# A later place in the planned order for two of GpSimd's products in a fused attention and state-space kernel

## The chip, the core and the metric

The kernel runs on one core of a Trainium2 chip. The metric is the device time of one execution in microseconds (us), the median of three runs. The core's engines are called by the profile's names: PE is TensorE (matmuls and transposes; PEld its weight loads), DVE is VectorE, ACT is ScalarE, POOL is GpSimd, SP is SyncE, which here issues the DMAs. Each engine works through its own instructions strictly in the order in which they were written; an instruction whose inputs are not there holds up all that stand behind it on its engine.

## The reference

The input is a batch of 8 images of 56 x 56 points with 192 channels. Two residual layers follow each other. The first is an attention layer over the points, with depthwise convolutions in front. The second, in which nearly all the time goes, is a selective state-space layer:

```
x = x + L0_conv(_gn(x))                       # group norm, convolutions, 3-head attention
x = x + L1_conv(_gn(x))                       # group norm, then for each image:
  xz = in_proj(x); xa, z = split(xz)          # 384 channels each
  xc = silu(conv3x3(xa))
  4 directions over the 3136 points (rows, columns, and both backwards), per direction:
    dts, Bs, Cs = split(x_proj(u))            # 12 + 16 + 16 rows
    delta = softplus(dt_proj(dts) + bias)
    for every point l, every channel, every one of 16 states n:
      h = exp(delta * A[n]) * h + delta * u * B[n, l]
      y = sum over n of h[n] * C[n, l]
  y = layernorm(sum of 4 directions) * silu(z); out_proj(y)
```

## The kernel before, in words

**The tiles.** An image is cut into 7 chunks of 448 points (T = 448), the 384 channels into 3 blocks of 128 (NJ = 3). With 8 images and 4 directions there are 8 x 4 x 7 = 224 chunk steps, and with 16 states each 3584 pairs (i, n) of a chunk step i and a state n. All of it is float32.

**What happens to one pair (i, n).** POOL multiplies `du`, the product of delta and u for the chunk, by a row of B that a DMA has spread over the partitions: this makes the input tile `h` of 128 x 1344 (`inputs_made`, L1127). ACT makes the three decays `da` (`decays`, L1141). DVE runs three scans along the points, in place in `h` (`scans`, L1158), and a small reduction copies the last column into `newc`, the carry for the next chunk (`carries`, L1180). Then `h` has to be multiplied by a row of C and added up over the states, and this is done in one of two ways:

- For 11 of the 16 states (13 in the last image) PE turns `h` (`turned`, L1204), ACT scales it by columns of C while it leaves PSUM (`scaled`, L1220), and PE turns it back and adds it up in the PSUM tile `y` (`back`, L1238).
- For the others POOL does it (`by_pool`): three products of `h` with the row of C, `cb`, one per channel block (L1257). `BY_POOL` puts the states in groups: (2, 5), (8, 10), (13) in the first seven images and (2, 7), (12) in the last. The first of a group writes its product into the tile `yp`; the next multiplies in place and POOL adds it to `yp` (L1261). PE then adds `yp` to `y` (`summed`, L1276). There is one `yp`.

At the end of a chunk step DVE adds `y` into `yacc` (`evicted`, L1293). There are seven buffers for `h` (`HBUFS = 7`), two for `du`, for delta and for `cb`, five for the rows of B, two for `da`.

**delta and u.** `prepared` makes delta for the next chunk step with PE, ACT and DVE (L1067 to L1086, the last one L1086, three times). Then POOL multiplies it into `du` (L1090), once per chunk step, and the chunk step is entered in `chunks`, on which the generators of the row loads, of the decays and of the inputs wait.

**Beside the scans** run the front of the next image (attention, projections, convolutions: `front`, `x_proj`) and the end of the last one (`finish`, with one POOL product at L988 per chunk). The front of the first image runs alone, before the first scan.

**What sets the order.** A list scheduler (`Sched`) plays the program in a model while the instructions are written. Every activity is a generator that asks for (engine, cost, cells read, cells written). The model knows when each cell was written, and with `LATE` how long after an instruction's end it can be used. Among all that could go next it takes the one with the smallest start less rank (`run`), and writes the instruction. The start is the latest of the stage's own start, its inputs and what is still read of its outputs, plus `HOP` = 0.04, and of the time at which the engine is free. The ranks are 0.39 for `by_pool`, 0.3 for `prepared`, 0.0 for `inputs_made`. The model's times steer only the order: on the chip each instruction waits for semaphores, and nothing else.

Where PE would be idle in the model for more than 0.45 us while `y` is being added up, the scheduler writes filler matmuls by `zeros` into an unused part of `y` (`keep_busy`, L1372), which keep PE's clock up; each counts 0.225 us in the model and each is an instruction that the chip carries out.

Of the kernel before, what the change touches and what calls it, by code (L numbers as in the profile page):

```python
# [10 lines left out]
ALU = mybir.AluOpType  # L11
# [10 lines left out]
T = 448  # L22
# [12 lines left out]
NJ = DIN // 128  # L35
# [18 lines left out]
PE, ACT, DVE, POOL, SP = range(5)  # L54
LATE = (0.17, 0.08, 0.09, 0.06, 0.0)
HOP = 0.04
MARGIN = 3.0
URGENT = 0.9


# [4 lines left out]
def t_mm(n):  # L65
    return n * 0.00171
# [6 lines left out]
def t_act(n):  # L73
    return 0.17 + n * 0.00085


def t_dve(n):
    return 0.07 + n * 0.00105


def t_pool(n):
    return 0.13 + n * 0.00214
# [82 lines left out]
class Sched:  # L165
# [17 lines left out]
    def resume(self, s, value=None):  # L183
        was, self.now = self.now, s
        try:
            s.req = s.gen.send(value)
        except StopIteration:
            s.done, s.req = True, None
        self.now = was

    def join(self, stages):

        me = self.now
        yield lambda: all(s.done for s in stages)
        me.start = max([me.start] + [s.end for s in stages])
# [7 lines left out]
    def give(self, s, t):  # L203
# [5 lines left out]
        if s.group is not None and e == PE:  # L209
            self.spent[s.group] = self.spent.get(s.group, 0.0) + cost  # L210
        end = t + s.req[4] + MARGIN if len(s.req) > 4 else end + LATE[e]
        for c in reads:
# [6 lines left out]
    def run(self, until=None):  # L219
        while True:  # L220
# [20 lines left out]
            for s in self.stages:  # L241
# [3 lines left out]
                if s.group in self.limit:  # L245
# [4 lines left out]
                    if spent < must:  # L250
                        rank = URGENT
                e, _, reads, writes = s.req[:4]
# [21 lines left out]
def kernel(  # L274
# [24 lines left out]
    nc = tc.nc  # L299
# [108 lines left out]
    sc = Sched()  # L408
# [57 lines left out]
    def dma(reads, writes, late, dst, src, after=()):  # L466
        yield SP, 0.07, reads, writes, late
        nc.sync.dma_start(dst, src)
        for t in after:
            t.free()  # L470
# [569 lines left out]
    chunks, brow, crow, das, states, news, ys = {}, {}, {}, {}, {}, {}, {}  # L1040
# [4 lines left out]
    def prepared():  # L1045

        for i, (b, k, c, _) in enumerate(steps):
            yield lambda: b in made and (k, c) in made[b]["k_ct"] and (k, c) in made[b]["k_rows"]
            m = made[b]
            cols = slice(c * T, (c + 1) * T)  # L1050
            dts = yield rdts[k // 2]
            yield from dma([m["k_rows"][k, c]], dts.c, 2.9, dts.ap[k // 2 * 64 + 1:k // 2 * 64 + 1 + R, :],
                           m["rows"][k][0:R, cols])
            ct = yield s2("ct_s", [TP, SUB, NST])
            yield from dma([m["k_ct"][k, c]], ct.c, 1.8, ct.ap, m["ct"][k][:, c * SUB:(c + 1) * SUB])
            dl = yield s2("dl_s", [128, NJ, T], parts=NJ)
            du = yield s2("du_s", [128, NJ, T], parts=2)
            yield from dma(m["k_xcs"][k % 2][c], du.c[:1], 5.5, du.ap, m["xcs"][k % 2][:, :, cols])


            for j in range(NJ):
                e = yield s2("e", [128, T])
                pdt = yield rprep
                k1, free = [Cell() for _ in range(3)], Cell()
                free.w = e.c[0].r
                yield PE, t_mm(T), dts.c, pdt.c
                nc.tensor.matmul(pdt.ap[:, :T], dtw[:, k % 2, j * 128:(j + 1) * 128], dts.ap,  # L1067
                                 start=True, stop=True)
                yield ACT, t_act(T), pdt.c + [free], [k1[0]]
                nc.scalar.activation(e.ap, pdt.ap[:, :T], AF.Abs)  # L1070
                yield ACT, t_act(T), [k1[0]], [k1[1]]
                nc.scalar.activation(e.ap, e.ap, AF.Exp, scale=-1.0)
                yield DVE, t_dve(T), pdt.c + [k1[1]], [k1[2]]
                nc.vector.scalar_tensor_tensor(dl.ap[:, j], pdt.ap[:, :T], 0.0, e.ap, ALU.max, ALU.add)  # L1074
                pdt.free()
                u = yield rprep
                k2 = [Cell() for _ in range(2)]
                yield ACT, t_act(T), [k1[1]], u.c + e.c
                nc.scalar.activation(u.ap[:, :T], e.ap, AF.Identity, bias=one)
                e.free()  # L1080
                yield DVE, t_dve(T), u.c + [k1[2]], [k2[0]]
                nc.vector.scalar_tensor_tensor(dl.ap[:, j], u.ap[:, :T], -1.0, dl.ap[:, j], ALU.add, ALU.subtract)  # L1082
                yield ACT, t_act(T), [k2[0]], [k2[1]]
                nc.scalar.activation(u.ap[:, :T], u.ap[:, :T], AF.Ln)
                yield DVE, t_dve(T), [k2[1], k2[0]], [dl.c[j]]
                nc.vector.tensor_tensor(dl.ap[:, j], u.ap[:, :T], dl.ap[:, j], ALU.subtract)  # L1086
                u.free()
            dts.free()
            yield POOL, t_pool(NJ * T), dl.c + du.c[:1], du.c[1:]
            nc.gpsimd.tensor_tensor(du.ap, dl.ap, du.ap, ALU.mult)  # L1090
            chunks[i] = (dl, du, ct)

    def skips():
# [72 lines left out]
    def over(i, n):  # L1166
        s = states[i, n]
        s[1] -= 1
        if s[1] == 0:
            states.pop((i, n))[0].free()  # L1170
# [73 lines left out]
    def by_pool():  # L1244

        for i, n in todo:
            if n not in by[i]:
                continue
            yield lambda: (i, n) in states and (i, n) in crow and i in news
            h, cbr = states[i, n][0], crow.pop((i, n))  # L1250
            first, last = by[i][n]
            if first:
                yp = yield s1("yp", [128, NJ, T], parts=NJ)
            to = yp if first else h
            for j in range(NJ):
                yield POOL, t_pool(T), [h.c[1 + j], news[i].c[n]] + cbr.c, [to.c[j]] if to is yp else [h.c[1 + NJ + j]]
                nc.gpsimd.tensor_tensor(to.ap[:, j], h.ap[:, j], cbr.ap, ALU.mult)  # L1257
            cbr.free()
            if to is h:
                yield POOL, t_pool(NJ * T), h.c[1 + NJ:] + yp.c, yp.c  # L1260
                nc.gpsimd.tensor_tensor(yp.ap, yp.ap, h.ap, ALU.add)  # L1261
            over(i, n)
            if last:
                yps.append((i, yp))
# [33 lines left out]
    with tc.manual_schedule():  # L1298
# [11 lines left out]
        with ExitStack() as es:  # L1310
# [15 lines left out]
            for g, rank in ((prepared, 0.3), (skips, 0.0), (row_loads, 0.25), (inputs_made, 0.0), (decays, 0.37),  # L1326
                            (scans, 0.16), (carries, 0.36), (turned, 0.37), (scaled, 0.38), (by_pool, 0.39),
                            (back, 0.4), (summed, 0.0), (evicted, 0.71)):
                sc.spawn(g(), rank, "scan")
# [114 lines left out]
```

## Time and profile before

| | us |
|---|---|
| median of three runs (18645.85 to 18656.8) | 18655.95 |
| span of the profiled execution, first to last instruction | 18641.6 |
| POOL busy | 16430.8 |
| PE busy (fillers of L1372: 1708.4 of it) | 16947.4 |
| DVE busy | 14715.5 |
| ACT busy | 14638.2 |
| mean granted PE clock, share of full | 0.978 |

The profile is of one execution. Its span is 14.4 us under the median of the runs, which also hold what lies around the instructions. Busy times are per engine and overlap; PE's are drawn out by the modelled ends of its matmuls. In a group of instructions the last column is the idle time of the engine just before them and what ended most of it. "A <- B" in a list of waits says that engine line A sat idle until B released it; "issue" as the releaser means that the profile shows nothing that it waited for.

### The profile page before, as it was taken

The page shows a single profiled execution, that of the slowest core. Times are in us where ns is not written, and L with a number is a line of the kernel's source. Part 1 is how long each engine was busy: PE and PEld are TensorE (multiplying, and loading weights), DVE is VectorE, ACT ScalarE, POOL GpSimd, SP SyncE. Part 2 cuts the span into 40 slices and gives each one's busy share as a digit, 9 for nine tenths or more (in the row PEclk, how much of TensorE's full clock was granted, in tenths as well). Part 3 has the DMA queues.
Part 4 walks back from the last instruction along what each step waited for, and adds up shares of the span by engine and source line. Part 5 has one row for each costly group of instructions (what it writes and reads, how often), then busy time and mean ns, then how long its engine had stood idle before and what let it go on. Part 6 is the DMA issues. An engine that isn't in the chain of part 4 may idle for free. (4 is left out here: it accounts for less than half of the span.)

```text
span 18641.6 us, 275449 instructions
## 1 busy us (share of the span) xinstructions
PE 16947.4 (91%) x97320; PEld 11601.9 (62%) x97320; DVE 14715.5 (79%) x19156; ACT 14638.2 (79%) x26598; POOL 16430.8 (88%) x7528
## 2 busy tenths in 40 slices
PE   8799999999989999899999999999899998999998
PEld 4465666655666566665666656665566655667776
DVE  2387787887878788787887888788787887879998
ACT  2378787787877878778787787878888787889998
POOL 0398898999989999899998999999999998999998
PEclk9899999999999999999999999999999999999999
DMA  1332334323343233323343323333333333342222
GB/s 53 112 94 79 82 103 126 85 82 95 102 118 85 81 95 109 114 82 80 100 112 108 83 77 108 109 105 81 83 104 111 104 83 84 101 114 86 82 81 66
DMA packets 1128349, 1750.85 MB, mean 94 GB/s; under 512 B 168516, under 2 KB 1110840, under 8 KB 1123896
## 3 DMA queue, kind: packets, MB, share of 16 engines
q1 hardware_dynamic: 1126968, 1733.23, 33.3%
q8 instruction: 770, 12.62, 0.3%
q14 instruction: 611, 5.01, 0.1%
HBM read 1545.05 MB, written 187.74 MB: 93 GB/s over the span
## 5 line engine op out<-in xcount | busy, mean ns | idle before, releaser
L1158 DVE TENSOR_TENSOR_SCAN h<-da,newc,h 128x448 f32<-128x448 f32 x9216 | 10171.1, 1137 | 1952.6 <-ACT da L1141 1012.6
L1127 POOL TENSOR_TENSOR h<-du_s,bb 128x1344 f32<-128x1344 f32 x3584 | 10816.3, 3051 | 272.1 <-PE ht L1204 185.5
L1141 ACT ACTIVATE da<-dl_s,acoef 128x448 f32<-128x448 f32 x10752 | 6741.5, 636 | 1207.6 <-DVE h L1158 1167.4
L1220 ACT ACTIVATE g<-ht,ct_s 112x384 f32<-112x384 f32 x10080 | 5529.3, 575 | 1119.8 <-PE ht L1204 974.5
L1238 PEld LDWEIGHTS y<-ident,g 112*128 112x128 f32 x30240 | 3304.6, 142 | 3162.9 <-ACT g L1220 2305.4
L1238 PE MATMUL y<-ident,g 112*128 112x112 f32 x30240 | 4586.8, 270 | 523.8 <-ACT g L1220 353.7
L1204 PE MATMUL ht<-ident,h 128*112 128x128 f32 x30240 | 4709.0, 275 | 160.7 <-DVE oT L721 68.1
L1204 PEld LDWEIGHTS ht<-ident,h 128*112 128x112 f32 x30240 | 3444.3, 135 | 753.4 <-issue 270.8
L1257 POOL TENSOR_TENSOR yp<-h,cb 128x448 f32<-128x448 f32 x1932 | 2147.1, 1142 | 371.8 <-PE y L1276 213.2
L1158 DVE TENSOR_TENSOR_SCAN h<-da,h 128x448 f32<-128x448 f32 x1536 | 1613.1, 1078 | 403.6 <-ACT da L1141 222.7
L1257 POOL TENSOR_TENSOR h<-h,cb 128x448 f32<-128x448 f32 x1260 | 1399.6, 1141 | 530.5 <-DVE newc L1180 265.8
L1276 PE MATMUL y<-yp,ident 128*128 128x448 f32 x3864 | 1750.2, 545 | 8.0 <-POOL yp L1257 4.7
L1372 PEld LDWEIGHTS y<-zeros 128*128 128x128 f32 x12624 | 1655.6, 198 | 86.7 <-issue 86.7
L1372 PE MATMUL y<-zeros 128*128 128x64 f32 x12624 | 1708.4, 273 | 0.0
L1090 POOL TENSOR_TENSOR du_s<-dl_s,du_s 128x1344 f32<-128x1344 f32 x224 | 682.3, 3046 | 906.0 <-DVE dl_s L1086 839.4
L1261 POOL TENSOR_TENSOR yp<-yp,h 128x1344 f32<-128x1344 f32 x420 | 1280.4, 3049 | 27.2
L454 PE MATMUL bank<-xa,dg 128*128 128x440 f32 (+2 forms) x3024 | 1263.1, 535 | 45.2 <-ACT g L1220 21.2
L758 PE MATMUL bank<-qT,kT 128*112 128x448 f32 x2352 | 1106.1, 576 | 134.3 <-ACT pT L708 47.0
L767 PE MATMUL bank<-pT,vt 112*128 112x448 f32 x2352 | 1008.0, 545 | 62.7 <-ACT pT L708 57.1
L708 ACT ACTIVATE pT<-bank,nsh 112x448 f32<-112x448 f32 x1176 | 740.2, 632 | 358.8 <-PE bank L758 202.0
L454 PE MATMUL bank<-band,dgq 96*96 96x440 f32 (+3 forms) x2016 | 842.1, 534 | 27.8 <-ACT hq L584 13.1
L1067 PE MATMUL prep<-dts,dtw 128*128 128x448 f32 x1344 | 662.4, 575 | 143.5 <-DVE dl_s L1086 130.4
(152 smaller groups left out, 12918.1 us busy)
## 6 DMA issues: line engine op xcount, KB each, us to landing
bb<-rows SPq DMA_DIRECT2D x3584, 224.0 KB
cb<-rows SPq DMA_DIRECT2D x1064, 224.0 KB
xt<-x1d SPq DMA_DIRECT2D x224, 336.0 KB
du_s<-xch SPq DMA_DIRECT2D x112, 672.0 KB
du_s<-xcw SPq DMA_DIRECT2D x112, 672.0 KB
xch<-xv SPq DMA_DIRECT2D x24, 1568.0 KB
xcw<-xw SPq DMA_DIRECT2D x168, 224.0 KB
xs<-xch SPq DMA_DIRECT2D x56, 672.0 KB
```

The source lines that it names most:

```text
L454: nc.tensor.matmul(out[:, o0:o1, a:b], lhs, img(lo, hi)[:, :, a + dx - 1:b + dx - 1], start=(t == TAPS[0]), stop=(t == TAPS[-1]))
L758: nc.tensor.matmul(ps.ap[:TP, :T], kts[h][:, kb * TP:(kb + 1) * TP], qh.ap, start=True, stop=True)
L1127: nc.gpsimd.tensor_tensor(h.ap, du.ap, bb.ap.unsqueeze(1).to_broadcast([128, NJ, T]), ALU.mult)
L1141: nc.scalar.activation(da.ap[:, :T], dl.ap[:, j], AF.Exp, scale=acoef[:, k * NJ + j, n:n + 1])
L1158: nc.vector.tensor_tensor_scan(h.ap[:, j, rev], da.ap[:, 0:T][:, rev], h.ap[:, j, rev], news[i - 1].ap[:, j, n:n + 1] if ci else 0.0, ALU. ...
L1204: nc.tensor.transpose(ht.ap[:TP, j * 128:(j + 1) * 128], h.ap[:, j, s * TP:(s + 1) * TP], ident)
L1220: nc.scalar.activation(g.ap, ht.ap[:TP, :DIN], AF.Copy, scale=ct.ap[:, s, n:n + 1])
L1238: nc.tensor.matmul(y["t"].ap[:, j, s * TP:(s + 1) * TP], g.ap[:, j * 128:(j + 1) * 128], ident[:TP, :TP], is_transpose=True, start=(n == 0 ...
L1257: nc.gpsimd.tensor_tensor(to.ap[:, j], h.ap[:, j], cbr.ap, ALU.mult)
L1261: nc.gpsimd.tensor_tensor(yp.ap, yp.ap, h.ap, ALU.add)
L1276: nc.tensor.matmul(y["t"].ap[:, j, :T], ident, yp.ap[:, j], start=False, stop=(y["left"][j] == 0))
L1372: nc.tensor.matmul(ybanks[:, 0, T:T + FILL], zeros, zeros[:, :FILL], start=False, stop=False)
```

## The change

A new generator `slack` waits until the cells named were planned, and then sets the start of the stage that calls it to at least 2.0 us after the time at which the model has them ready. It is used in two places: before the three products with a row of C (and the sum behind them), where it is counted from `newc`, and before the product of delta and u, counted from delta. The latter becomes a stage of its own, so `chunks[i]` is entered without waiting for the product to be written. No instruction's operands, cost or buffers change.

```diff
 MARGIN = 3.0
+SLACK = 2.0
 URGENT = 0.9
...
+    def slack(self, cells):
+
+        yield lambda: all(c.w is not None for c in cells)
+        self.now.start = max([self.now.start] + [c.w + SLACK for c in cells])
...
             dts.free()
-            yield POOL, t_pool(NJ * T), dl.c + du.c[:1], du.c[1:]
-            nc.gpsimd.tensor_tensor(du.ap, dl.ap, du.ap, ALU.mult)
+
+            def product(dl, du, k_du):
+                yield from sc.slack(dl.c)
+                yield POOL, t_pool(NJ * T), dl.c + du.c[:1], k_du
+                nc.gpsimd.tensor_tensor(du.ap, dl.ap, du.ap, ALU.mult)
+
+            sc.spawn(product(dl, du, du.c[1:]))
             chunks[i] = (dl, du, ct)
...
             yield lambda: (i, n) in states and (i, n) in crow and i in news
             h, cbr = states[i, n][0], crow.pop((i, n))
+            yield from sc.slack([news[i].c[n]])
             first, last = by[i][n]
```

## The prediction

> **What bounds the kernel now.** I read the page's busy times, the costliest groups, the busy times by stage, then the waits of POOL and DVE.
>
> ```profile
> PE 16947.4 (91%) x97320; PEld 11601.9 (62%) x97320; DVE 14715.5 (79%) x19156; ACT 14638.2 (79%) x26598; POOL 16430.8 (88%) x7528
> ...
> L1127 POOL TENSOR_TENSOR h<-du_s,bb 128x1344 f32<-128x1344 f32 x3584 | 10816.3, 3051 | 272.1 <-PE ht L1204 185.5
> L1257 POOL TENSOR_TENSOR yp<-h,cb 128x448 f32<-128x448 f32 x1932 | 2147.1, 1142 | 371.8 <-PE y L1276 213.2
> L1257 POOL TENSOR_TENSOR h<-h,cb 128x448 f32<-128x448 f32 x1260 | 1399.6, 1141 | 530.5 <-DVE newc L1180 265.8
> L1090 POOL TENSOR_TENSOR du_s<-dl_s,du_s 128x1344 f32<-128x1344 f32 x224 | 682.3, 3046 | 906.0 <-DVE dl_s L1086 839.4
> ```
>
> ```profile
> core 0: us, PE busy (x) PEld busy (x) DVE busy (x) ACT busy (x) POOL busy (x), PEclk, DMA share, GB/s
> 7700.00:10000.00 2300.00, 2091.97 (x11910) 1421.55 (x11910) 1857.80 (x2408) 1832.59 (x3326) 2112.88 (x976) 0.98 0.36 99
> 16900.00:18585.00 1685.00, 1549.68 (x11432) 1242.43 (x11430) 1542.01 (x1943) 1526.88 (x2868) 1630.04 (x687) 0.99 0.28 79
> ```
>
> In the middle of the run POOL is busy 2113 of 2300 us; PE's 2092 hold 185 of fillers (the same stage for L1372 alone), so its real work is 1907. In the last image, without a front beside it, POOL reaches 1630 of 1685. POOL is the fullest engine, and its work (16430.8 us) does not change, so the end moves with POOL's idle time. Of its 2211 us (span less busy) some 727 are the first L1090 waiting for the lone first front. What the change aims at is 902 before the products with C (371.8 + 530.5) and about 179 before L1090 (906.0 - 727).
>
> ```profile
> POOL h L1257 <- DVE newc L1180: 265.8, 124, 13.7
> POOL h L1257 <- issue: 250.7, 60, 10.1
> POOL yp L1257 <- PE y L1276: 213.2, 96, 11.2
> POOL h L1127 <- PE ht L1204: 185.5, 60, 9.1
> ```
>
> ```profile
> DVE h L1158 <- ACT da L1141: 1235.3, 1644, 5.8
> DVE h L1158 <- POOL h L1127: 1014.4, 313, 10.9
> ```
>
> The two engines wait for each other: POOL for carries from DVE's scans, DVE for POOL's inputs. One place:
>
> ```profile
> 9751.72 6.06 POOL L1127 TENSOR_TENSOR h<-du_s,bb 128x1344 f32<-128x1344 f32 x2
> 9765.37 3.32 POOL L1257 TENSOR_TENSOR h<-h,cb 128x448 f32<-128x448 f32 x3 [7.59 <-issue]
> 9768.77 3.04 POOL L1261 TENSOR_TENSOR yp<-yp,h 128x1344 f32<-128x1344 f32 x1
> ```
>
> POOL stands for 7.6 us before a product with C, and no input behind it can pass. When it goes on, product and sum take 6.4 us more before the next input.
>
> **What the change moves.** The order of instructions in the two builds shows the same work, and 617 more fillers (6929 for 6312). I call the number of inputs (L1127) that stand between state n's own input and its product with C the lead. Its mean goes from 2.91 to 3.35: of 1064 triples 433 stand later, 539 as before, 92 earlier. By state in the first seven images: state 2 +0.74, 5 +0.48, 8 +0.50, 10 +0.56 (1.71 to 2.27), 13 none; last image, state 7, +0.68. L1090 stands later in 85 of 224 steps, earlier in 40, on average by 0.32 inputs.
>
> *Products with C.* From the trace's POOL instructions in order I took the gap before each triple (898 us in all). Upper bound of the gain: an input moved ahead fills the gap with its 3.05 us, or all of a smaller gap. The gaps so capped sum by state to 271 us (5), 173 (8), 72 (10), 22 (2), 65 (13), 11 (7 of the last image); by the shifts that is 130 + 87 + 40 + 16 - 1 + 7 = 279 us. The other bound: price each lead at the mean gap that groups of that state and lead have now. State 5 stalls 4.38 us at lead 2, 1.38 at 3, 1.29 at 4, 6.94 at 5; state 8 0.46, 0.61, 2.54, 2.68 at 2 to 5. Long leads stall longer, because they stand where all else is late. With the new counts of leads (one not seen now at the price of the next) the first seven images' sum goes from 888 to 1038: a loss of 150. I take the gain where it can be kept: 572 of the 898 us are at leads up to 3, and there a stalled POOL also leaves DVE short; at 4 and more POOL is far ahead and an added input would run into the seven buffers. 279 x 572/898 = **-178 us**.
>
> *delta and u.* The gaps, capped in the same way, are 139 us; x 0.32 = **-45**; ends 0 and -139. That `chunks[i]` is entered earlier moves row loads and decays up in the plan. bb and cb loads had landed in time but for 66.6 and 1.5 us of POOL's waits, and decays have two buffers only: I take nothing, and 20 either way out of these 68. L1090's cover is the old chunk's remaining inputs: 4.76 of them on average (5.08 before), about 14 us.
>
> *Buffers.* Longer leads hold `h` longer. POOL's waits before inputs are 272.1 us now; grown as the lead (3.35/2.91, 15%) that is **+41**, ends 0 and 100.
>
> *Fillers.* In the timeline a filler's two passes start 0.11 us apart, 0.222 us each filler: 617 are 137 us of PE. What is queued behind them is PE's next turn, for which ACT waits. In the chain that ended last, L1372 has 0.5% of the span, 93 us, in the 2377 us that the chain covers; fillers fill about 415 us there (358.6 of the last image's stage and 636/2300 of the 203.2 of the one before), so 22% of them are on the path: **+31**, ends 0 and 137.
>
> *Sum:* -178 - 45 + 41 + 31 = -151 us. The span goes from 18641.6 to about 18491; the median lies 14 us above it: 18505.
>
> *A rule that speaks against it.* In the window 8954 to 8967 a DVE copy stands beside four inputs in a row:
>
> ```profile
> 8954.76 11.94 POOL L1127 TENSOR_TENSOR h<-du_s,bb 128x1344 f32<-128x1344 f32 x4
> 8956.04 10.69 DVE L431 COPY mean<-gm 96x2 f32<-96x2 f32 x1
> ```
>
> L431 takes 0.165 us at its shortest; here it ends as POOL's run ends. Summed over L431, L674, L678 and L464 (median less minimum, times count) such holds cost DVE 24 + 40 + 39 + 8 = 111 us; longer unbroken runs of inputs could add as much again, and I leave that to the range. The Trainium skill (SBUF — State Buffer, "Who interferes with whom") says that copies and `tensor_scalar` may use a port pair shared with GpSimd, and that the later one is blocked until the other's instruction ends. By the page a hold could not outlast one input of 3.05 us and the change would add nothing here; the row has 10.69, over four.
>
> **Rivals.** *Much faster (10%).* What counts is DVE's hunger, not POOL's stall. Behind a state-10 product with its sum DVE is short 834 of some 1077 us (gaps before the first scan of an input that had just come). Lead 0 costs 8.6 us a time, 1 to 3 about 4. Moved by 0.56 in 196 groups, at up to 3.05 us, that is -335 in place of -178; with the other terms -308: 18348. For it: in most of these cases POOL had not stalled in the 10 us before. Against it: POOL's work stays the same, and only its idle time can shrink.
>
> *No difference (12%).* Each gap filled comes back before the next input, as a wait for `h` buffers (L1127 <- L1204), or the shift is too small to do what it says (539 of 1064 not moved): 0 - 45 + 31, about 18642.
>
> *Slower (31%).* POOL is stalled because the rest is late, not because of its own order. Then a longer lead only keeps `h` and the one `yp` longer, PE's sum (L1276) comes later, and the next first-of-group product waits for it (213.2 us already). The place is states 5 and 8 at leads of 4 and more, which rise from 127 to 227 of 392 groups; the price is the +150 above; it decides as soon as these groups keep their mean gap of about 2.3 us. 150 - 45 + 41 + 31 = +177: 18833.
>
> **How the numbers follow.** Forecast 47%, much faster 10%, no difference 12%, slower 31%. 0.2% (37 us) is about what a measurement of this kernel can tell from no change; faster by more 0.57, within 0.12, slower by more 0.31. The forecast's own range, each term half way to its ends and these taken together as independent (root of squares: 73 down, 177 up), is 18432 to 18682. The whole range goes down past 18348 by half of L1090's remaining 94 us, to 18300, and up past 18833 to 18850, which leaves out the upper half of the slower case's fillers and the ends that would have to meet.
>
> **What would show it.** Right: POOL's idle time before L1257 falls from 902 to about 725, before L1090 by some 45, before L1127 it rises by about 40; DVE's wait for L1127 falls below 1014. Busy POOL stays at 16430. Wrong: idle before L1257 stays near 900 with the same sizes at states 5 and 8, or what leaves it stands again before L1127; or PE's fillers move the chain, seen as L1372's share well above 0.5%.

## The result and the profile after

The changed kernel takes 18765.64 us (median of four runs, 18758.39 to 18770.82) against 18656.38 us before (18645.85 to 18659.1): **1.006 times the time, interval 1.0046 to 1.0074**. It is slower by some 109 us, where 18505 was forecast. The profiled execution's span is 18768.3 us, 126.7 more than before, at the same granted clock (0.978). That execution took 18769.94 us in all, 1.7 us more than its span. The rest of the 14 us that the forecast added to its span, and the step from 109 to 126.7, come from comparing single executions with medians.

The groups of the products in the page after (columns as before: busy, mean of one, idle time just before them and what ended most of it); L1138 is the old L1127, L1269 the old L1257, L1099 the old L1090:

```profile
PE 17102.1 (91%) x98554; PEld 11774.9 (63%) x98554; DVE 14664.7 (78%) x19156; ACT 14627.4 (78%) x26598; POOL 16429.2 (88%) x7528
...
L1138 POOL TENSOR_TENSOR h<-du_s,bb 128x1344 f32<-128x1344 f32 x3584 | 10817.7, 3053 | 611.7 <-PE ht L1215 275.0
...
L1269 POOL TENSOR_TENSOR yp<-h,cb 128x448 f32<-128x448 f32 x1932 | 2146.6, 1143 | 609.7 <-PE y L1288 498.9
...
L1269 POOL TENSOR_TENSOR h<-h,cb 128x448 f32<-128x448 f32 x1260 | 1399.3, 1142 | 203.8 <-DVE newc L1191 161.2
...
L1099 POOL TENSOR_TENSOR du_s<-dl_s,du_s 128x1344 f32<-128x1344 f32 x224 | 682.6, 3047 | 775.6 <-DVE dl_s L1092 773.5
```

POOL's work is the same to 2 us. Where the change aimed, its idle time went: the in-place products (state 5 and 10) fell from 530.5 to 203.8, the product of delta and u from 906.0 to 775.6, which is little more than the 725 of the first front. But the idle time before the inputs rose from 272.1 to 611.7 and that before the first-of-group products from 371.8 to 609.7. The list of POOL's waits says on what:

```profile
POOL yp L1269 <- PE y L1288: 498.9, 177, 15.4
POOL h L1138 <- PE ht L1215: 275.0, 82, 9.1
POOL h L1138 <- DMA bb<-rows: 252.1, 63, 10.6
POOL h L1269 <- DVE newc L1191: 161.2, 71, 13.9
```

Before, the first three were 213.2, 185.5 and 66.6, the last 265.8. By kind of instruction, from the rows of the two pages and the trace:

| POOL's idle time before | before | after | change |
|---|---|---|---|
| products with C | 902 | 813 | -89 |
| delta times u (without the first) | 179 | 50 | -128 |
| inputs | 272 | 612 | +340 |
| end stage's product | 44 | 52 | +8 |
| sum | 1397 | 1528 | +131 |

With some 3 us less at other places that is the span's 126.7 and the 1.6 us by which POOL was busy less, to within a microsecond. Nearly all of it is in the seven images that have a front beside them: from an image's first input to the next one's, they sum to 15916 us before and 16041 after; the last image, from its first input to its last, takes 1871.7 and 1872.7. DVE, too, waits longer for both of its partners (1235.3 and 1014.4 before):

```profile
DVE h L1169 <- ACT da L1152: 1407.5, 1710, 7.0
DVE h L1169 <- POOL h L1138: 1129.6, 295, 19.4
```

### The profile page after: what moved, and what is told of

The parts are those of the page before. It is cut to its first block, busy times and chain, and to the rows that moved or that the text cites. A ratio compares the mean times of both kernels' runs of the same rounds, so it can differ in the third digit from the quotient of the medians.

```text
span 18768.3 us, 278080 instructions
## 1 busy us (share of the span) xinstructions
PE 17102.1 (91%) x98554; PEld 11774.9 (63%) x98554; DVE 14664.7 (78%) x19156; ACT 14627.4 (78%) x26598; POOL 16429.2 (88%) x7528
## 5 line engine op out<-in xcount | busy, mean ns | idle before, releaser
L1138 POOL TENSOR_TENSOR h<-du_s,bb 128x1344 f32<-128x1344 f32 x3584 | 10817.7, 3053 | 611.7 <-PE ht L1215 275.0
L1269 POOL TENSOR_TENSOR yp<-h,cb 128x448 f32<-128x448 f32 x1932 | 2146.6, 1143 | 609.7 <-PE y L1288 498.9
L1384 PE MATMUL y<-zeros 128*128 128x64 f32 x13858 | 1877.9, 277 | 0.0
L1384 PEld LDWEIGHTS y<-zeros 128*128 128x128 f32 x13858 | 1824.4, 201 | 79.1 <-issue 78.7
L1269 POOL TENSOR_TENSOR h<-h,cb 128x448 f32<-128x448 f32 x1260 | 1399.3, 1142 | 203.8 <-DVE newc L1191 161.2
L1099 POOL TENSOR_TENSOR du_s<-dl_s,du_s 128x1344 f32<-128x1344 f32 x224 | 682.6, 3047 | 775.6 <-DVE dl_s L1092 773.5
```

Source lines behind the costliest of these rows:

```text
L1138: nc.gpsimd.tensor_tensor(h.ap, du.ap, bb.ap.unsqueeze(1).to_broadcast([128, NJ, T]), ALU.mult)
L1384: nc.tensor.matmul(ybanks[:, 0, T:T + FILL], zeros, zeros[:, :FILL], start=False, stop=False)
```

## The experiments

Each time is a median, with its ratio to the kernel before on the same chip and the 95% interval. The runs were made on several chips, on which the kernel before takes 18644 to 18656 us; where two of the runs are compared below, it is by how far each is from the kernel before on its own chip (+109 us for the changed kernel).

| run | edit | us | ratio | interval | fillers |
|---|---|---|---|---|---|
| changed kernel | both places, 2.0 us | 18765.6 | 1.0060 | 1.0046 to 1.0074 | 6929 |
| e1 | 2.0 us for C alone | 18801.7 | 1.0084 | 1.0069 to 1.0100 | 6908 |
| e2 | 2.0 us for delta times u alone | 18732.2 | 1.0046 | 1.0029 to 1.0063 | 6513 |
| e3 | changed, two yp | 18675.9 | 1.0017 | 1.0008 to 1.0026 | 6736 |
| e4 | changed, three cb | 18821.6 | 1.0095 | 1.0080 to 1.0110 | 6899 |
| e5 | changed, 630 fillers fewer | 18775.9 | 1.0068 | 1.0053 to 1.0083 | 6299 |
| e6 | before, 632 fillers more | 18653.5 | 1.0003 | 0.9994 to 1.0012 | 6944 |
| e7 | before, no fillers | 18948.9 | 1.0156 | 1.0139 to 1.0173 | 0 |
| e8 | changed, no fillers | 19100.1 | 1.0241 | 1.0226 to 1.0256 | 0 |
| e9 | before, two yp | 18577.1 | 0.9966 | 0.9953 to 0.9979 | 6413 |
| e10 | before, product as own stage, 0 us | 18649.9 | 1.0005 | 0.9995 to 1.0014 | 6312 |
| e11 | before, rank of C products 0.0 | 19096.2 | 1.0243 | 1.0228 to 1.0258 | 5728 |
| e12 | changed, rank of PE's sums 0.5 | 18687.5 | 1.0022 | 1.0013 to 1.0032 | 7148 |
| e13 | before, HOP 0.045 | 18732.0 | 1.0046 | 1.0030 to 1.0063 | 6602 |
| e14 | before, POOL cost + 0.001 | 18716.8 | 1.0040 | 1.0025 to 1.0055 | 6612 |
| e15 | changed, 1.9 us | 18906.0 | 1.0141 | 1.0126 to 1.0156 | 6992 |
| e16 | changed, 2.1 us | 18882.1 | 1.0127 | 1.0112 to 1.0142 | 7051 |
| e17 | before, HOP 0.035 | 18803.2 | 1.0080 | 1.0063 to 1.0097 | 6707 |
| e18 | changed, 0.5 us | 18723.8 | 1.0037 | 1.0024 to 1.0050 | 6531 |

### The two halves: e1 and e2

e1 writes the product of delta and u as before; e2 drops the other line:

```diff
-            sc.spawn(product(dl, du, du.c[1:]))            # e1, with the function
+            yield POOL, t_pool(NJ * T), dl.c + du.c[:1], du.c[1:]
+            nc.gpsimd.tensor_tensor(du.ap, dl.ap, du.ap, ALU.mult)
...
-            yield from sc.slack([news[i].c[n]])            # e2
```

> The 2.0 us are kept for the products with C alone; delta times u is written as before. Theory A (the one yp buffer and the two cb buffers turn the later place of the C products into new waits): the loss is all in this half, so at least the changed kernel's 18766, some 18760 to 18890, with POOL's wait for PE's sum before the first-of-group products near 500 us. Theory B (the 617 more fillers on PE are the loss): 18766 only if the fillers come with this half, time in step with their number at 0.22 us each. Theory C (delta times u as a stage of its own, with row loads and decays planned earlier, is the loss): 18620 to 18670.

> The 2.0 us are kept for delta times u alone, as a stage of its own; the products with C are placed as before. Theory A: no loss here, and the 120 us of idle time that went before this product in the changed kernel show as a gain, 18540 to 18650. Theory B: near 18656, fillers near 6312. Theory C: slower, 18740 to 18790.

Both halves lose alone, and together they lose no more than the first by itself (1.0060 against 1.0084). All three theories fail on one of the two.

e1 reaches what the change aimed at and is 157 us slower all the same: before the products with C POOL's idle time falls from 902 to 564 us, nearly twice the gain that was forecast, but before delta times u it rises from 179 to 399 and before the inputs from 272 to 538. Two of its three largest waits, 839.4 and 185.5 us before, show where it went:

```profile
POOL du_s L1097 <- DVE dl_s L1092: 1029.3, 90, 727.2
POOL h L1134 <- PE ht L1211: 351.0, 102, 9.3
```

In e2 the aimed wait is gone: POOL's idle time before the product fell from 179 to 66 us. The products with C, which nothing had moved on purpose (their mean lead is 2.96, 2.91 before), took 180 us more (902 to 1082), most of it at state 8 (244 to 381):

```profile
POOL du_s L1099 <- DVE dl_s L1092: 764.6, 12, 730.3
POOL yp L1268 <- PE y L1287: 472.3, 131, 13.5
```

So the wait for PE's sum of `yp`, 213.2 us before, can grow without a delay of the C products.

### The scarce buffers: e3, e4, e9 and e12

```diff
-                yp = yield s1("yp", [128, NJ, T], parts=NJ)                  # e3, e9
+                yp = yield s1("yp", [128, NJ, T], bufs=2, parts=NJ)
...
-                cbr = yield s2("cb", [128, T])                               # e4
+                cbr = yield s2("cb", [128, T], 3)
...
-                            (back, 0.4), (summed, 0.0), (evicted, 0.71)):    # e12
+                            (back, 0.4), (summed, 0.5), (evicted, 0.71)):
```

To make room for the second `yp`, e3 and e9 also take `ot` from the ring of `sz`, and use `lnones` (with `-SCALE * DIN` behind it) in place of `ones`.

> The changed kernel with two yp buffers in place of one (room for it is made by putting the output rows of the end stage in its own freed sz buffer and by dropping one constant). Theory A: POOL's wait for PE's sum falls from 499 us to under 50 and the time by 150 to 300, to 18460 to 18620, below the kernel before. Theory B: the wait may fall, the time stays at 18720 to 18770 unless fillers fall too. Theory C: 18740 or more.

> The kernel before with two yp buffers (the same room made as in e3): the control to e3. If the one yp buffer is why the later place loses (theory A), it must matter less here, where its wait is 213 us and not 499: at most 50 us faster, 18600 to 18650, so that the later place costs little once there are two. Theory E (what the plan itself loses: the planned idle time of PE, of which the fillers written are the count, comes out on the chip whether they run or not): 6413 fillers, 101 more x 0.225 = +23, 18650 to 18700.

> The changed kernel with three buffers for the rows of C in place of two. Theory A: the rows of B that stand behind a held-up load of a row of C in SP's queue come in time, POOL's wait for them falls from 252 us to 70 or less, and the time by 80 to 185, to 18580 to 18690. Theory B and C: within 30 us of 18766.

> The changed kernel with the rank of PE's sums of yp raised from 0.0 to 0.5, so that they stand first in the plan as soon as they can. Theory A: POOL's wait for the sum falls from 499 us below 250, the time to 18600 to 18700. Theory E: 7148 fillers, 836 more than before, x 0.225 = +188: 18800 to 18870.

With two `yp` POOL's wait for PE's sum falls from 498.9 to 32.8 us, as theory A said, and the loss from 109 to 31 us; theory A had expected a time below the kernel before. POOL's wait for the carries rises from 161.2 to 512.2. DVE's wait for POOL's inputs more than halves (1129.6 before this edit), and its wait for ACT's decays grows in its place (1407.5):

```profile
DVE h L1169 <- ACT da L1152: 1838.1, 1926, 5.8
DVE h L1169 <- POOL h L1138: 483.2, 226, 5.7
```

The waits of POOL in e3 read:

```profile
POOL h L1269 <- DVE newc L1191: 512.2, 144, 16.1
POOL h L1138 <- PE ht L1215: 235.7, 77, 9.1
POOL h L1138 <- DMA bb<-rows: 219.7, 64, 11.3
```

e9 is the control: the kernel before gains 67 us from the same buffer, so that with two `yp` the later place still loses 18675.9 - 18577.1 = 99 us. That speaks against the one `yp` as the cause, but each of the two is a new order and one draw; e13 to e17 show how far orders differ. e12, which puts the sums first, halves the wait (498.9 to 263.0) and gets 66 us back: the time lies where theory A had it and far below theory E's, the wait 13 us above theory A's. It has no such control.

In e4 the third `cb` does what theory A said at its place: the gap before the input of state 9, whose row of B stands in SP's queue behind state 8's row of C, falls from 186 to 6 us (47 in the kernel before), and the wait for `bb` from 252.1 to 6.5. The time, which theory A had at 18580 to 18690, rises by 68 us, and other waits take its place:

```profile
POOL yp L1269 <- PE y L1288: 550.1, 187, 14.4
POOL h L1138 <- PE ht L1215: 410.4, 121, 9.2
```

### The fillers: e5 to e8

```diff
-                while True:
+                for z in range(10 ** 9):
                     yield PE, T_FILL, [], []
-                    nc.tensor.matmul(ybanks[:, 0, T:T + FILL], zeros, zeros[:, :FILL], start=False, stop=False)
+                    if z % 11:              # e5; e6 writes one, and a second if z % 10 == 0; e7, e8 none
+                        nc.tensor.matmul(ybanks[:, 0, T:T + FILL], zeros, zeros[:, :FILL], start=False, stop=False)
```

> The changed kernel, every instruction planned in the same order, but each eleventh filler is not written: 6299 in place of 6929, about the number before. Theory B (the fillers are the loss): 630 x 0.22 = up to 139 us back, 18620 to 18690. Theory A (the one yp buffer) and theory D (the order itself: each stall cured shows again elsewhere): 18735 to 18765, at most the 31 us that the prediction put on the path.

> The kernel before, same order, with a second filler written behind every tenth: 6944 in place of 6312, about the number after. Theory B: 18740 to 18790, the changed kernel's time. Theories A and D: 18645 to 18690.

> The kernel before, same order, with no fillers written at all (the plan still counts them). With the next run it compares the two orders alone. All theories: the granted clock of PE may fall without fillers and cost time; with the clock unchanged, theory B expects 18640 less a large part of 6312 x 0.22 = 1400 us, D and A some 0 to 350 less (22% of them on the path).

> The changed kernel, same order, with no fillers written at all. Theory B: within 30 us of the kernel before without fillers. Theories A and D: still slower than that one by 80 to 150.

Theory B falls: with the order kept, 630 fillers fewer give nothing back and 632 more cost nothing that can be measured. It looks as if these fillers stand where PE waits on the chip, too. Without any, the two orders still differ, by 19100.1/18948.9 = 1.008, though the granted clocks differ a little there (0.941 and 0.935 in the profiled executions), and some of it may be that. The two kernels do the same work, and the fillers are not the loss: the order is.

### Does the plan foretell it, and does the split matter? e10 and e11

```diff
-                yield from sc.slack(dl.c)                                     # e10, with the line at by_pool
...
-                            (scans, 0.16), (carries, 0.36), (turned, 0.37), (scaled, 0.38), (by_pool, 0.39),
+                            (scans, 0.16), (carries, 0.36), (turned, 0.37), (scaled, 0.38), (by_pool, 0.0),    # e11
```

> The kernel before with delta times u as a stage of its own and the next chunk entered early, but no 2.0 us at all. If the 2.0 us made the loss of e2, this is the kernel before: 18630 to 18670. If the split does (theory C, and theory E by its 6531 fillers, 219 more x 0.225 = +49): 18690 to 18740.

> The kernel before with the rank of the products with C lowered from 0.39 to 0.0, no slack: another way to a later place, in which a product gives way only to work that can start no later. The plan writes 5728 fillers, 584 fewer. Theory E: 584 x 0.225 = 131 us faster, 18490 to 18560. Theory A (any later place makes the yp buffer late): 18700 or more, POOL's wait for PE's sum above 300 us.

The 6531 fillers in e10's expectation were a wrong count: its trace holds 12624 filler records, 6312 fillers, as before, and its gaps by state are those of the kernel before (437 at state 5, 240 at state 8; 440 and 241 before). The split by itself leaves the order and the time as they were. e11 has the fewest planned fillers and the worst ratio, and e9 and e12 miss theory E's times too: the plan's idle time foretells nothing here (theory E falls). Theory A's words on e11 come true (18700 or more, a wait above 300 us). Its mean lead is 4.14, its granted clock lower (0.965), and POOL waits most for `h` buffers, 185.5 us before:

```profile
POOL h L1127 <- PE ht L1204: 525.0, 185, 7.3
POOL yp L1257 <- PE y L1276: 350.6, 104, 11.3
```

### The later place, or any other order? e13 to e18

```diff
-HOP = 0.04
+HOP = 0.045                              # e13; 0.035 in e17
...
-    return 0.13 + n * 0.00214
+    return 0.131 + n * 0.00214           # e14
...
-SLACK = 2.0
+SLACK = 1.9                              # e15; 2.1 in e16, 0.5 in e18
```

> The kernel before with HOP = 0.045 in place of 0.04 in the model: no later place, but the order changes (6602 fillers in place of 6312). Theory F (the kernel before stands at a good draw among many orders, and any disturbance of the plan loses some 0.3 to 1%): 18700 to 18820. Theory G (it is the later place that loses): within 35 us of the kernel before, 18610 to 18690.

> The kernel before with 0.131 in place of 0.13 us as the fixed part of a GpSimd product's cost in the model: no later place, another order (6612 fillers). Theory F: 18700 to 18820. Theory G: 18610 to 18690.

> The kernel before with HOP = 0.035 in place of 0.04: a third order without a later place. Theory F (any disturbance of the plan loses): 18690 to 18760, as for the other two. Theory G (only the later place loses, the other two were chance): within 35 us of 18645.

> The changed kernel with 1.9 in place of 2.0 us. Theory F: anywhere from 18650 to 18880, over 40 us from the changed kernel or from the next run. Theory G: within 25 us of the changed kernel, 18740 to 18790.

> The changed kernel with 2.1 in place of 2.0 us. Theory F: as for 1.9, the two over 40 us apart from each other or from the changed kernel. Theory G: within 25 us of the changed kernel, 18740 to 18790.

> The changed kernel with 0.5 in place of 2.0 us. If the loss beyond the disturbance goes with the size of the delay, this one is near the neutral draws, 18690 to 18760; if having the delay at all costs, it is with 1.9 and 2.1 us, above 18800.

Three numbers that mean nothing for the chip, with no later place, lose 0.46, 0.40 and 0.80%. A tenth of a microsecond either way takes the change's 0.60 to 1.41 and 1.27%. So theory G falls, and theory F fits in the main, though e15, e16 and e17 lie above the times it gave: orders scatter, all three neutral ones are slower than the kernel before, and the change's loss lies inside what they lose. That the kernel before stands at a good place among the orders is likely by three draws out of three, not more. The three draws near 2 us average 1.09%, the neutral ones 0.55%, and 0.5 us (0.37%) is with the neutral ones. That points to a cost of the later place beyond the disturbance, about half a per cent; with three draws each, and 0.60 and 0.80 crossing over, it is not shown.

The same scatter bears on e1 to e4, e9, e11 and e12. Each of them is a new order, and a difference in time of up to 0.8% between two orders can't be put down to the edit by one draw. What these runs do show is where POOL's idle time went. e5 to e8 and e10 keep the order and are free of this.

What the later place does is seen in where POOL is idle. In the neutral e17 it waits before the products, as in the kernel before:

```profile
POOL h L1257 <- DVE newc L1180: 414.3, 136, 12.0
POOL yp L1257 <- PE y L1276: 320.5, 104, 9.7
POOL h L1257 <- issue: 315.7, 80, 13.9
POOL h L1127 <- PE ht L1204: 139.7, 47, 9.0
```

In e15 (1.9 us) it waits before the inputs and before the first of a group:

```profile
POOL yp L1269 <- PE y L1288: 485.0, 162, 13.3
POOL h L1138 <- DMA bb<-rows: 272.6, 73, 12.0
POOL h L1138 <- PE ht L1215: 265.4, 67, 9.5
POOL h L1269 <- DVE newc L1191: 164.0, 69, 12.1
```

POOL's idle time before the inputs is 612, 684 and 692 us at 2.0, 1.9 and 2.1 us, and 229 to 294 in the three neutral orders (272 before). The places differ more than the sums: over the four kinds of the table above these are 1528, 1662 and 1632 us, against 1482 to 1559 in the neutral orders and 1397 before.

## Why the prediction was wrong

- **The step that failed** is the first: "so the end moves with POOL's idle time", with the four terms priced each on its own as if the rest of the order stood still. The identity is true (126.7 us of span, 128.3 of idle time, 1.6 less of work), but it is no price: a stall that goes at one place comes back at the next. e1 shows it best: the products with C gave up 338 us of idle time, more than was forecast, and the kernel lost 157 us. e2, e3 and e4 show it with other waits. In e3 DVE waits less for POOL and more for ACT. That POOL's idle time is what is left when DVE, ACT and PE have set the pace is argued from this, not shown. The page before had a sign of it: in the chain of work that ended last POOL has 1% of the span, less than three others, though that chain covers the last 2377 us alone.

```profile
ACT 4%; DVE 4%; PE 3%; issue 1%; POOL 1%; DMA 0%; POOLq 0%; ACTq 0%; SPq 0%; DVEq 0%
```

- *Products with C*, -178: measured -89. State 5 fell by 300 us (440 to 140), more than the 130 of the upper bound, state 10 from 80 to 64; state 8 rose from 241 to 519. At leads up to 3 the idle time fell by 282 us, at longer leads it rose by 193: the term took the first and left the second out.
- *delta and u*, -45: -128, near its far end of -139; the lead says less than thought.
- *Buffers*, +41 with ends 0 and 100: +340. This is the term that was most mis-sized. It scaled the waits with the mean lead and left out two things: the rows of B (66.6 to 252.1 us), which stand behind the loads of C's rows in SP's queue, as e4 showed; and waits that end with the front's work on DVE (73 us at L513 and L516, 3.5 before). The `h` buffers alone, 185.5 to 275.0, were inside it.
- *Fillers*, +31: 0 (e5, e6). The row of the chain, 22% of them on the path, was no price either.
- **The slower rival** had the side and part of the place (state 8, the `yp`, PE's sum; state 5 fell). At leads of 4 and more in states 5 and 8 the idle time rose about as it said (127 groups at 2.30 us, then 227 at 1.96), but it fell by more elsewhere, so the products' gaps shrank in place of growing by 150. "Much faster" fails as well: DVE's wait for inputs rose. *No difference* was nearest in mechanism, since the gaps came back before the next input, but it named the `h` buffers, which are 90 of the 340 us. The prediction's own sign of being wrong came true: what left L1257 stood again before L1127.
- **No rival said** that any other order could lose as much. The page could not have shown it; a second, neutral order would have.
- *The rule on the shared port.* Longer runs of inputs were to hold DVE longer. Taken one by one, the holds at the four lines sum to 172 us before (the prediction's 111 came from medians) and 114 after, so they did not grow in sum; but one lasted 12.294 us. The Trainium skill (SBUF — State Buffer, "Who interferes with whom") has the block last for the other's one instruction; POOL's longest here is 3.4 us. The trace before has both: 11 of the 24 subtractions on kT (L674) take 2.28 to 2.31 us and end some 0.4 us after the POOL product then running, as the page has it, but six of the 16 copies at L431 take 10.69 to 10.73 and end with a run of four inputs, as it has not. No wait for a semaphore stands before these copies, so instructions on the chip wait for more than semaphores.

**Open:** what makes one order 0.8% better than another, and whether 2 us cost anything of their own. e9 is faster than both kernels (0.9966), but one order with two `yp` is one draw, and no neutral order was run around it: its 67 us are measured, and their cause is not.

## What to carry to other kernels

Where a scheduler writes the order, compare a change with a neutral disturbance of the plan before giving it a cause: here a number of 0.04 turned into 0.045 cost 0.46%. Where engines wait for each other in a ring, as POOL, DVE, ACT and PE do here, the idle time in front of one instruction is not a price; ask who would be late next, in every queue that the moved work stands in, SP's too. Each buffer held longer here (`h`, `cb`, `yp`) showed up as a wait for the next one.

## What had not been expected of the hardware

A tenth of the fillers on PE, more or fewer, was free as long as the order stayed (632 more, of 0.222 us each: 1.0003, interval 0.9994 to 1.0012), and all of them together are worth 1.56%: without them the mean granted clock of PE is 0.941 in place of 0.978.

```profile
core 0: 18957.3 us, clock 0.941
```
